# A graph layer and a mixture of experts on one core: statistics moved between folds, a table written in longer pieces, read-backs paced anew

## The chip, the cores and the metric

The kernel runs on one core of a Trainium2 chip. The metric is device time in microseconds of one execution, median of several runs. The core has five instruction streams that run beside each other and wait for one another on semaphores: TensorE (PE in the profile; PEld is its weight load), VectorE (DVE), ScalarE (ACT), GpSimd (POOL) and SyncE (SP), which here only issues DMAs. Each stream works strictly in its own order. Sixteen DMA engines move data between HBM and the on-chip memories.

## The reference, cut to what matters

```python
deg = jnp.maximum(segment_sum(ones, dst), 1.0); norm = deg ** (-0.5)
# graph layer: 6250 nodes, 106250 edges sorted by dst, 256 features
h = norm * (layernorm(x) @ W.T + b)
x = x + norm * segment_sum(h[src], dst)
# feed-forward layer: 8 experts, 256 -> 1024 -> 256, best 2 of 8 for each node
y = layernorm(x)
scores = y @ Wg.T + bg
top, idx = top_k(scores, 2);  p = softmax(top)
out = x + sum over the 2 chosen e of p_e * (relu(y @ W1[e].T + b1[e]) @ W2[e].T + b2[e])
```

The inputs are `x`, `src`, `dst` and the weights. Nothing is computed on the host; edges are only laid out as 831 chunks of 128.

## The kernel before, in words

The nodes are cut into 49 tiles of 128, tile `t` holding nodes `128 t` to `128 t + 127`, one a partition. The function `in_order` does everything; a second path, `any_order`, is taken only if a flag `g.bad` says that some assumption on the order of the edges or experts did not hold.

**First stage (lines 180 to 415), in an order written out by hand.** It makes a table `ftable` in HBM with one row of 1 KB (512 numbers in 16 bits) for each node, from which the edges are later gathered. For this it needs, of each node, mean and variance (`look(n)`, line 253: the next `n` tiles' statistics, one VectorE instruction each) and the degree. Degrees are counted on TensorE: `tally(c0, c1)` (line 268) multiplies one-hot forms of the chunks `c0` to `c1` into count tiles, one for each group of seven tiles; three such count tiles exist at a time, so a fourth waits until VectorE has copied the first away. `fold_counts(k0, k1)` (line 361) copies the counts of groups `k0` to `k1` on VectorE (`counted`) and spreads them over the partitions on TensorE (`degrees`, L296). `moments` and `columns` turn statistics and degrees into a factor and an offset for each node (VectorE, with one square root on ScalarE); `scaled(k)` applies them (ScalarE, from group 3 on partly VectorE) and rounds to 16 bits (L346, ScalarE); `rest(k)` (L349, VectorE) makes the low half of each row; `stored(k)` (L351) writes the group's 128 x 7 rows to the table with one DMA on SP, the last group with two. The tiles `tab` of three groups exist at a time.

Since TensorE and VectorE work in program order, a fold on TensorE stands behind all count matmuls of the tally written ahead of it, and whatever VectorE has next after a fold waits for it. Behind the last `rest`, VectorE makes small constants (lines 407 to 415). The memory of this stage is then reused, so the next stage's first masks wait for the last store of the table.

**Middle (lines 893 to 909).** One step `s` for each chunk of 128 edges: `gather` (L433) fetches 128 table rows with an indirect DMA on GpSimd, by the node numbers in `g.src`; VectorE makes a mask; TensorE adds the rows up (L447). Around this, at steps fixed by the tables `tasks` and `FINAL`, finished tiles are put through the linear layer, routed to two experts (`route`) and sorted into queues in HBM (`sort`, L665; `send`). The function `next_piece` puts in one piece of the feed-forward layer for each step: 56 FFN steps of 256 rows of one expert (the last five of 128). An FFN step is `up` (L780), `down` (L794) and the result `y` (L798, VectorE), written to `fyq` in HBM by SP.

**Tail (lines 910 to 996).** The same loop goes on without gathers: `read_back` (L855) fetches with an indirect DMA on GpSimd, for one tile and one of its two experts, 128 rows of results; `add_in` (L863, VectorE) adds them, 14 steps after the read or later; after some adds `store` writes four finished tiles out, from GpSimd's queue. `DONE` says how many tiles are complete after which FFN step: `(54, 46)` opens tiles up to 45 for reading once step 54 is through. A read that is opened by FFN step n waits for the writes of steps up to n alone. The table `bounds`, made from `DONE`, lets `flag` (L935) check on chip that this held for the data. `flag` counts on VectorE, sums over partitions with one matmul on TensorE (L951) 8 steps later and sets `g.bad` (L954) 4 steps after that. Tiles not opened before the last FFN step are read at the end, all reads in a row (line 990), and then added and stored one tile at a time. At last every engine loads `g.bad` and branches.

Of the kernel before, what the change touches and what calls it, by code (L numbers as in the profile page):

```python
# [10 lines left out]
I32 = mybir.dt.int32  # L11
# [4 lines left out]
OP = mybir.AluOpType  # L16
# [3 lines left out]
P = 128  # L20
N = 6250
NT = 49
# [4 lines left out]
NC = 831  # L27
# [13 lines left out]
USUAL = len(FOLLOWS) + 9  # L41
# [12 lines left out]
GROUP = 7  # L54
# [1 line left out]
SHIFT = 1.0 / 16  # L56

DONE = ((40, 31), (42, 33), (44, 34), (45, 35), (46, 37), (47, 38), (48, 39), (49, 40), (50, 42), (51, 43),
        (52, 44), (53, 45), (54, 46), (USUAL - 1, NT))
LATER = 1 << 17  # L60


# [70 lines left out]
def in_order(ctx: ExitStack, tc: tile.TileContext, g: Shared, srcT, dstT, low):  # L133
# [36 lines left out]

    most = keep.tile([P, NE], F32, name="most")
    zeros = keep.tile([P, D], F32, name="zeros")

    kept = {w: (WINDOWS[w - 1][0] % P, WINDOWS[w][0] - WINDOWS[w - 1][0]) for w in range(1, len(WINDOWS))}
    keeps = {key: keep.tile([P, 1], F32, name=f"keep{j}") for j, key in enumerate(sorted(set(kept.values())))}
# [4 lines left out]
    with (tc.manual_schedule(), tc.tile_pool(name="fdeg", bufs=2) as deg,  # L180
# [118 lines left out]
        def moments(k0, k1):  # L299

            t0, t1 = k0 * GROUP, k1 * GROUP
            n = t1 - t0
            v = deg.tile([P, 2, n], F32, name="v")
            nc.vector.tensor_scalar(v[:, 1], pds.pop(k0), 1.0, None, op0=OP.max)

            twice = deg.tile([P, n], F32, name="twice")
            nc.vector.tensor_add(twice, st[:, t0:t1, 1], st[:, t0:t1, 4])
            apart = deg.tile([P, n], F32, name="apart")
            nc.vector.tensor_sub(apart, st[:, t0:t1, 1], st[:, t0:t1, 4])
            nc.vector.scalar_tensor_tensor(apart, apart, 0.25, apart, op0=OP.mult, op1=OP.mult)  # L310
            nc.vector.tensor_add(v[:, 0], st[:, t0:t1, 2], st[:, t0:t1, 5])
            nc.vector.scalar_tensor_tensor(v[:, 0], v[:, 0], 1.0 / D, apart, op0=OP.mult, op1=OP.add)
            nc.vector.tensor_scalar(v[:, 0], v[:, 0], EPS, None, op0=OP.add)
            r = deg.tile([P, 2, n], F32, name="rs")
            nc.scalar.activation(r, v, AF.Sqrt)
            cols[k0] = twice, v, r
# [32 lines left out]
            nc.vector.tensor_sub(tab[k][:, a:b, D:2 * D], hf[k][:, a:b, :], tab[k][:, a:b, 0:D])  # L349

        def stored(k, a=0, b=GROUP):  # L351
            nc.sync.dma_start(table[(k * GROUP + a) * P:(k * GROUP + b) * P, :].rearrange("(t p) d -> p t d", p=P),
                              tab[k][:, a:b, :])


# [5 lines left out]
        def fold_counts(k0, k1):  # L361
            for k in range(k0, k1):
                counted(k)
            degrees(k0, k1)
# [3 lines left out]
        ones(256, NC)  # L368
        tally(0, 256)
        fold_counts(0, 1)  # L370
        moments(0, 1)
        look(4)
        columns(0, 1)
        scaled(0)
        tally(256, 460)
        look(10)
        fold_counts(1, 3)
        moments(1, 3)
        look(4)
        columns(1, 3)  # L380
        scaled(1)
        scaled(2)
        last_parts(0)
        tally(460, 730)
        look(10)
        fold_counts(3, 5)
        last_parts(1)
        moments(3, 5)
# [1 line left out]
        columns(3, 5)  # L390
        scaled(3)
        scaled(4)
        tally(730, NC)
        last_parts(2)
        look(7)
        fold_counts(5, 7)
        moments(5, 7)
        columns(5, 7)
# [3 lines left out]
        last_parts(4)  # L402
        last_parts(5)
        last_parts(6, ((0, 4), (4, GROUP)))


        nc.vector.tensor_scalar(g.ident, g.jp, 0.0, None, op0=OP.is_equal)
# [23 lines left out]
    def gather(c):  # L431
        rows[c] = rowpool.tile([P, 2 * D], F16, name="rows")
        nc.gpsimd.indirect_dma_start(  # L433
            out=rows[c], out_offset=None, in_=table[:, :],
            in_offset=bass.IndirectOffsetOnAxis(ap=g.src[:, c:c + 1], axis=0))

    def mask(c):
        masks[c] = work.tile([P, P], F16, name="mask", bufs=MASKS + 3)
# [454 lines left out]
    with tc.manual_schedule():  # L893
        with rowp as rowpool:
            for c in range(AHEAD):
                gather(c)
            for c in range(MASKS):
                mask(c)
            for s in range(NC):
                if s + AHEAD < NC:  # L900
                    gather(s + AHEAD)
                if s + MASKS < NC:
                    mask(s + MASKS)
                add_up(s)
                for fn, args in tasks.pop(s, []):
                    fn(*args)
                next_piece(s)
                if s % 4 == 0 and earliest.get(done + 1, NC) <= s:
                    next_piece(s)
        with tc.tile_pool(name="ftail", bufs=2) as pool:  # L910
            s = NC
            pend = []
            plan = list(DONE)
            found = list(DONE)
            got = asked = allowed = stored = 0
            latest = 0
            since = {}

            def take():
                nonlocal got, stored  # L920
                t, j, yb = pend.pop(0)[1]
                add_in(t, j, yb)
                got += 1
                if got == 2 * stored + 11:
                    store(stored, stored + 4, nc.gpsimd)
                    stored += 4

            def find():

                while found and sought > found[0][0]:  # L930
                    step, t1 = found.pop(0)
                    results(DONE[-len(found) - 2][1] if len(found) + 1 < len(DONE) else 0, t1,
                            float(P + (step + 1) * FT))

            def flag():  # L935


                late = work.tile([P, NT, 2], F32, name="late", bufs=1)
                missed = work.tile([P, 2], F32, name="missed")
                nc.vector.tensor_tensor(late, at, bounds, op=OP.is_ge)  # L940
                nc.vector.tensor_reduce(missed[:, 0:1], late, op=OP.add, axis=mybir.AxisListType.XY)
                nc.vector.tensor_reduce(missed[:, 1:2], most, op=OP.max, axis=mybir.AxisListType.X)
                nc.vector.tensor_scalar(missed[:, 1:2], missed[:, 1:2], float(SLOTS), None, op0=OP.is_gt)
                nc.vector.tensor_add(missed[:, 0:1], missed[:, 0:1], missed[:, 1:2])
                nc.vector.tensor_add(missed[:, 0:1], missed[:, 0:1], g.outside)
                ones = work.tile([P, 1], F32, name="ones")
                nc.vector.memset(ones, 1.0)
                for _ in range(8):
                    yield
                pm = psp.tile([1, 1], F32, name="pt", bufs=1)  # L950
                nc.tensor.matmul(pm, missed[:, 0:1], ones, start=True, stop=True)  # L951
                for _ in range(4):
                    yield
                nc.vector.tensor_scalar(g.bad, pm, 1.0, None, op0=OP.min)  # L954

            flagged = None
            while done < USUAL or tasks or len(plan) > 1 or asked < 2 * allowed or pend:
                for fn, args in tasks.pop(s, []):
                    fn(*args)
                if s > all_sent:  # L960
                    if chosen < min(USUAL, done + 4):
                        run(choose(chosen))
                        chosen += 1
                    elif chosen == USUAL and flagged is None:
                        flagged = True
                        in_parts(s + 1, flag)
                    if loaded2 < min(loaded1, done + 3):
                        load_second(loaded2)
                        loaded2 += 1
                    if loaded1 < min(chosen, done + (cur >= HB) + 3):  # L970
                        load_first(loaded1)
                        load_rows(loaded1)
                        loaded1 += 1
                was = done
                next_piece(s)
                if done > was:
                    since[was] = s
                find()
                if len(plan) > 1 and done > plan[0][0] and s >= since.get(plan[0][0], 0) + 4 \
                        and asked == 2 * allowed:  # L980
                    latest, allowed = plan.pop(0)
                if asked < 2 * allowed and s % (4 if s > all_sent else 2):
                    pend.append((s, read_back(pool, rowat, asked // 2, asked % 2, latest)))
                    asked += 1

                if pend and (done == USUAL or len(pend) == WAITING - 1 or s >= pend[0][0] + 14):
                    take()
                s += 1

            last = [read_back(pool, rowat, t, j) for t in range(allowed, NT) for j in range(2)]  # L990
            if stored < allowed:
                store(stored, allowed, nc.sync)
            for t, j, yb in last:
                add_in(t, j, yb)
                if j:
                    store(t, t + 1, nc.sync if t % 2 else nc.scalar)
# [495 lines left out]
```

## Time and profile before

| what | value |
|---|---|
| median of five runs (lowest, highest) | 1325.51 us (1320.11, 1327.92) |
| the profiled execution, its span | 1316.57 us, 1314.7 us |
| busy: TensorE, VectorE, GpSimd, ScalarE | 89%, 73%, 69%, 30% of the span |
| first gather, last gather | 76.6 us, 1119.6 us |
| first read-back, last read-back | 1134.99 us, 1304.48 us |
| bytes moved, mean rate | 326.02 MB, 248 GB/s |

A row of the profile's timeline gives the start and the duration in microseconds from the span's start, the engine, the line of the kernel, the operation with its output and inputs, how many instructions it merges, and in brackets how long the engine was idle before it and what ended that. A row of the windows gives, for a stretch of time, its length, the busy time of TensorE, its weight load, VectorE, ScalarE and GpSimd with the count of instructions, the granted TensorE clock, the busy share of the DMA engines and the GB/s they moved. Durations on GpSimd are rough. Names such as `rows<-ftable,src` are output and inputs.

### The profile page before, as it was taken

What the parts mean: (1) busy time and instruction counts of PE and PEld (TensorE: products, weight loads), DVE (VectorE), ACT (ScalarE), POOL (GpSimd) and SP (SyncE); (2) the same over time, 40 slices, a digit from 0 to 9 for tenths busy, and PEclk for the clock granted to TensorE, in tenths of its full rate; (3) what the DMA queues carried; (4) which work ended last, traced back from release to release, by engine and by line L of the source; (5) the groups of instructions that cost most, each with busy time, mean ns of one, the idle gap of its engine ahead of it and who ended that gap; (6) DMA issues with size and microseconds to landing.
All of it is one profiled execution on the core that took longest, in us unless ns stands there. A gap on an engine that the chain in (4) does not pass through costs nothing. (4 is left out here: it accounts for less than half of the span.)

```text
span 1314.7 us, 23752 instructions
## 1 busy us (share of the span) xinstructions
PE 1167.2 (89%) x6208; PEld 920.4 (70%) x6208; DVE 962.7 (73%) x5230; ACT 396.4 (30%) x936; POOL 900.6 (69%) x994
## 2 busy tenths in 40 slices
PE   5449886999899989999999999999999999899983
PEld 5437654767677767778777777777777777688873
DVE  7932667766878887887888887888777776875652
ACT  3712322222233232323333323333232323223221
POOL 2057777777777777777777777777777777447753
PEclk9999777999999999999999999999999999999987
DMA  9353456878788878897878787878888787689993
GB/s 321 121 158 106 121 137 206 260 244 268 242 240 275 273 234 260 258 328 253 269 249 281 240 284 225 290 233 280 274 253 289 221 289 244 222 292 399 310 351 120
DMA packets 159082, 326.02 MB, mean 248 GB/s; under 512 B 26724, under 2 KB 105528, under 8 KB 144600
## 3 DMA queue, kind: packets, MB, share of 16 engines
q1 hardware_dynamic: 111948, 196.14, 43.1%
q0 software_dynamic: 46176, 127.59, 32.9%
q8 instruction: 51, 0.84, 0.3%
q14 instruction: 95, 0.78, 0.2%
q10 hardware_dynamic: 812, 0.68, 0.2%
HBM read 268.88 MB, written 55.42 MB: 247 GB/s over the span
## 5 line engine op out<-in xcount | busy, mean ns | idle before, releaser
L433 POOL DMA_INDIRECT rows<-ftable,src x831 | 790.3, 951 | 321.8 <-issue 96.4
L780 PE MATMUL ph<-xT,w 128*128 128x256 f32 (+1 forms) x1792 | 447.1, 380 | 31.3 <-ACT xT L768 31.0
L794 PE MATMUL py<-w,hid 128*128 128x256 f32 x1712 | 431.9, 382 | 3.3 <-DVE y L798 3.3
L780 PEld LDWEIGHTS ph<-xT,w 128*128 128x128 f32 x1792 | 331.8, 195 | 104.5 <-ACT xT L768 41.0
L794 PEld LDWEIGHTS py<-w,hid 128*128 128x128 f32 x1712 | 325.6, 191 | 75.9 <-DVE y L798 3.5
L447 PE MATMUL ps<-rows,mask 128*128 128x512 f16 x831 | 320.3, 399 | 33.6 <-DMA rows<-ftable,src 29.0
L785 ACT ACTIVATE hid<-ph,w 128x256 f32<-128x256 f32 (+1 forms) x448 | 183.3, 460 | 250.3 <-PE ph L780 171.0
L440 DVE TENSOR_SCALAR mask<-col_b,rel 128x128 f16<-128x128 bf16 x831 | 207.4, 269 | 45.9 <-PE ps L447 42.3
L855 POOL DMA_INDIRECT yb<-fyq,rowat x98 | 94.8, 968 | 66.8 <-issue 26.7
L529 ACT ACTIVATE whole<-rolled 32x256 f32<-32x256 f32 (+2 forms) x156 | 64.4, 413 | 214.2 <-DVE rolled L524 213.4
L447 PEld LDWEIGHTS <-mask 128*128 128x128 f16 x831 | 87.8, 106 | 56.7 <-issue 25.6
L798 DVE TENSOR_TENSOR y<-py,w 128x256 f32<-128x256 f32 x107 | 45.3, 423 | 94.6 <-PE py L794 94.5
L521 DVE SCALAR_TENSOR_TENSOR rolled<-rolled,keep,ps 128x256 f32<-128x256 f32 x149 | 70.4, 473 | 24.3 <-PE ps L447 20.3
L863 DVE SCALAR_TENSOR_TENSOR xr<-yb,prob,xr 128x256 f32<-128x256 f32 x98 | 45.3, 482 | 49.9 <-DMA yb<-fyq,rowat 49.0
L665 PE MATMUL px<-slots,h 128*128 128x256 f32 x196 | 57.4, 418 | 17.0 <-DVE slots L644 14.6
L524 DVE TENSOR_TENSOR rolled<-ps,rolled 128x256 f32<-128x256 f32 x150 | 63.7, 424 | 5.2
L665 PEld LDWEIGHTS px<-slots,h 128*128 128x128 f32 x196 | 36.9, 201 | 36.8 <-DVE slots L644 24.5
L605 ACT ACTIVATE ex<-ex 128x1 f32<-128x1 f32 x49 | 9.9, 203 | 174.2 <-DVE ex L604 174.2
L666 ACT ACTIVATE ordered<-px 128x512 f32<-128x512 f32 x49 | 31.0, 633 | 88.0 <-issue 48.6
L552 DVE SCALAR_TENSOR_TENSOR xr<-pt,norm,xr 128x256 f32<-128x256 f32 x49 | 23.6, 482 | 42.0 <-PE pt L544 41.9
L544 PE MATMUL pt<-gw,uT 128*128 128x264 f32 x196 | 53.4, 397 | 0.0
L768 ACT ACTIVATE xT<-xs 128x512 f32<-128x512 f32 (+1 forms) x56 | 36.2, 647 | 47.2 <-DMA xs<-fhq 46.8
(183 smaller groups left out, 1133.0 us busy)
## 6 DMA issues: line engine op xcount, KB each, us to landing
w<-in_W SPq DMA_DIRECT2D x56, 1152.0 KB
w<-in_W SPq DMA_DIRECT2D x56, 1028.0 KB
fhq<-ordered SPq DMA_DIRECT2D x392, 64.0 KB
fyq<-y SPq DMA_DIRECT2D x107, 128.0 KB
rows<-ftable,src POOLq DMA_INDIRECT x831
xs<-fhq SPq DMA_DIRECT2D x51, 256.0 KB
out<-xr POOLq DMA_DIRECT2D x11, 512.0 KB
xr<-in_x SPq DMA_DIRECT2D x6, 896.0 KB
```

The costliest lines, as they stand in the source:

```text
L433: nc.gpsimd.indirect_dma_start(out=rows[c], out_offset=None, in_=table[:, :], in_offset=bass.IndirectOffsetOnAxis(ap=g.src[:, c:c + 1], ax ...
L440: nc.vector.tensor_scalar(masks[c], g.col_b[:, r:r + P], g.rel[:, c:c + 1], None, op0=OP.is_equal)
L447: nc.tensor.matmul(sums[w], masks.pop(c), rows.pop(c), start=(c == chunks[0]), stop=(c == chunks[-1]))
L521: nc.vector.scalar_tensor_tensor(new, rolled, keeps[kept[w]], ps[:, 0:D], op0=OP.mult, op1=OP.add)
L524: nc.vector.tensor_add(new, ps[:, D:2 * D], new)
L529: nc.scalar.activation(whole[t][p0:p1, :], new[p0:p1, :], AF.Copy)
L544: nc.tensor.matmul(pl, uT[:, k, :], gw[:, k, :], start=(k == 0), stop=(k == 1))
L665: nc.tensor.matmul(px[:, k, :], h2s[t][:, k * P:(k + 1) * P], slots[t], start=True, stop=True)
L780: nc.tensor.matmul(ph[:, b % 2, :n], w1[:, k * H + b * P:k * H + (b + 1) * P], f["xT"][:, k, :n], start=(k == 0), stop=(k == 1))
L785: nc.scalar.activation(f["hid"][:, b - 1 + i, :n], ph[:, i, :n], AF.Relu, bias=w1[:, 2 * H + b - 1 + i:2 * H + b + i])
L794: nc.tensor.matmul(f["py"], f["hid"][:, b, a * P:(a + 1) * P], f["w2"][:, b * D:(b + 1) * D], start=(b == 0), stop=(b == HB - 1))
L855: r = nc.gpsimd.indirect_dma_start(out=yb, out_offset=None, in_=yq[0:P + (upto + 1) * FT, :], in_offset=bass.IndirectOffsetOnAxis(ap=where ...
```

## The change

- The 49 statistics are made in other places: eight behind the first fold of counts (instead of seven ahead of the last), then 2, 6, 4, 3, 12 and 7 where there were 4, 10, 0, 4, 10 and 7.
- The second and third fold stand 20 and 30 chunks later in TensorE's order, the last tally is shorter by 30.
- The table's rows are numbered by partition first: node `128 t + p` stands in row `49 p + t`, so that one partition's seven rows of a group lie side by side. The gathers' row numbers are made from `g.src` by three VectorE instructions on 128 x 831 whole numbers, behind the last `rest`.
- While tiles are still being sorted, one read-back is issued in four steps instead of one in two.
- 47 tiles instead of 46 are opened once FFN step 54 is through.
- The flag's matmul and its last instruction stand behind the last FFN step, not in the middle of step 52.

```diff
-        (52, 44), (53, 45), (54, 46), (USUAL - 1, NT))
+        (52, 44), (53, 45), (54, 47), (USUAL - 1, NT))
...
+    rowof = keep.tile([P, NC], I32, name="rowof")
...
-            nc.sync.dma_start(table[(k * GROUP + a) * P:(k * GROUP + b) * P, :].rearrange("(t p) d -> p t d", p=P),
+            nc.sync.dma_start(table[:, :].rearrange("(p t) d -> p t d", p=P)[:, k * GROUP + a:k * GROUP + b, :],
                               tab[k][:, a:b, :])
...
         fold_counts(0, 1)
+        look(8)
         moments(0, 1)
-        look(4)
+        look(2)
         columns(0, 1)
         scaled(0)
-        tally(256, 460)
-        look(10)
+        tally(256, 480)
+        look(6)
         fold_counts(1, 3)
+        look(4)
         moments(1, 3)
-        look(4)
+        look(3)
         columns(1, 3)
         scaled(1)
         scaled(2)
         last_parts(0)
-        tally(460, 730)
-        look(10)
+        tally(480, 760)
+        look(12)
         fold_counts(3, 5)
...
-        tally(730, NC)
+        tally(760, NC)
         last_parts(2)
-        look(7)
         fold_counts(5, 7)
...
+        nc.vector.tensor_scalar(part, g.src, P - 1, None, op0=OP.bitwise_and)
+        nc.vector.tensor_scalar(part2, g.src, 7, None, op0=OP.arith_shift_right)
+        nc.vector.scalar_tensor_tensor(rowof, part, float(NT), part2, op0=OP.mult, op1=OP.add)
...
-            in_offset=bass.IndirectOffsetOnAxis(ap=g.src[:, c:c + 1], axis=0))
+            in_offset=bass.IndirectOffsetOnAxis(ap=rowof[:, c:c + 1], axis=0))
...
-                for _ in range(8):
+
+                while done < USUAL:
                     yield
                 pm = psp.tile([1, 1], F32, name="pt", bufs=1)
                 nc.tensor.matmul(pm, missed[:, 0:1], ones, start=True, stop=True)
-                for _ in range(4):
-                    yield
                 nc.vector.tensor_scalar(g.bad, pm, 1.0, None, op0=OP.min)
...
-                if asked < 2 * allowed and s % (4 if s > all_sent else 2):
+                if asked < 2 * allowed and (s % 4 if s > all_sent else s % 4 == 0):
```

## The prediction

> **What bounds the kernel now.** I read the profile's page first, then the answer on the table tile, the timeline of the first 92 us, the same stretch in 1 us windows, and the timeline of the last 200 us. The page's costliest group and the tile's answer say that GpSimd sets the length of the middle:
>
> ```profile
> L433 POOL DMA_INDIRECT rows<-ftable,src x831 | 790.3, 951 | 321.8 <-issue 96.4
> ...
> L433 POOL DMA_INDIRECT rows<-ftable,src x831: 942/946/1184, 76.6 to 1119.6; - x167
> ```
>
> 831 gathers start between 76.6 and 1119.6 us, 1.257 us apart; one is 0.946 us and the gap behind it 0.30 us (the timeline's rows), so 830 x 1.25 = 1037 of those 1043 us are plain succession. The middle can hardly shrink, but it moves as a whole with the first gather. The kernel is thus three pieces: until the first gather, 1043 us, and the tail.
>
> The first piece ends so (timeline, then windows; the last two columns of a window are the busy share of the 16 DMA engines and GB/s):
>
> ```profile
> 32.61 0.17 DVE L304 TENSOR_SCALAR v<-pd 128x14 f32<-128x14 f32 x1 [2.31 <-PE pd L296]
> ...
> 67.13 1.70 ACT L346 ACTIVATE tab<-hf 128x1792 f16<-128x1792 f32 x1 [1.48 <-DMA ftable<-tab]
> 68.86 2.09 DVE L349 TENSOR_TENSOR tab<-hf,tab 128x1024 f16<-128x1024 f32 x2 [1.02 <-ACT tab L346]
> ...
> 75.54 1.57 DVE L440 TENSOR_SCALAR mask<-col_b,rel 128x128 f16<-128x128 bf16 x9 [3.46 <-DMA ftable<-tab]
> ...
> 76.56 1.09 POOL L433 DMA_INDIRECT rows<-ftable,src  x1 [68.05 <-DVE mask L440]
> ```
> ```profile
> 67.00:68.00 1.00, 0.00 (x0) 0.00 (x0) 0.83 (x1) 0.87 (x1) 0.00 (x0) 1.00 1.03 353
> 68.00:69.00 1.00, 0.00 (x0) 0.00 (x0) 0.14 (x1) 0.82 (x1) 0.00 (x0) 1.00 1.02 328
> ...
> 74.00:75.00 1.00, 0.00 (x0) 0.00 (x0) 0.00 (x0) 0.00 (x0) 0.00 (x0) 1.00 0.94 323
> 75.00:76.00 1.00, 0.00 (x0) 0.03 (x1) 0.46 (x3) 0.00 (x0) 0.00 (x0) 1.00 0.01 2
> ```
>
> Read there: VectorE is done at 72.1 and idles 3.46 us; from 67.0 to 74.95 the DMA engines do nothing but the last 2.75 MB of the table at 346 GB/s (7.95 us). VectorE also idles 3.50 us at 22.57 and 2.31 us at 32.61 for the counts.
>
> In the tail GpSimd reads results back, each 1.25 us, and VectorE adds them in program order, so an add whose read is late holds the FFN result `y` behind it:
>
> ```profile
> 1174.53 0.81 POOL L870 DMA_DIRECT2D out<-xr  x1 [13.45 <-DVE xr L863]
> ...
> 1254.86 0.48 DVE L863 SCALAR_TENSOR_TENSOR xr<-yb,prob,xr 128x256 f32<-128x256 f32 x1 [5.43 <-DMA yb<-fyq,rowat]
> ...
> 1257.86 6.57 PE L794 MATMUL py<-w,hid 128*128 128x256 f32 x16 [3.31 <-DVE y L798]
> ...
> 1298.21 0.97 POOL L855 DMA_INDIRECT yb<-fyq,rowat  x1 [4.30 <-DMA fyq<-y]
> ...
> 1304.48 0.95 POOL L855 DMA_INDIRECT yb<-fyq,rowat  x1 [0.30 <-issue]
> ```
>
> After the last `y` has landed (1298.21) six reads follow one another, the sixth at 1304.48; its add ends at 1307.83 and the span at 1314.7.
>
> **Part 1, statistics and folds.** Same 49 statistics (0.335 us each), other places. I replay VectorE's order with the rows' durations. Eight now stand behind the first fold: 19.07 to 21.76, inside the 3.50 us idle; `v` stays at 22.57. Two instead of four before the first columns: these end 0.7 us earlier, 25.6. Six more to 27.6; the second count closes at 28.8 on TensorE, so both are folded at 29.2, and four more end at 30.6. But TensorE now runs 30 more count matmuls (0.032 us each) before it folds: `v` at 33.6, not 32.61, and VectorE idles 3.0 us there. With three instead of four statistics the columns end at 37.2 (36.5 before). Twelve instead of ten delay the fold of counts 3 and 4 to 43.5; TensorE needs that buffer for its seventh count, then has 58 instead of 28 matmuls left (2.0 us) and the fold: `v` at 46.2 (44.36). Columns end at 51.1 (49.26). Now the seven statistics that stood at 53.1 (2.38 us) are gone: counts 5 and 6 are folded at 54.97 (55.43). Net gain 0.46 us; most of the filled idle time comes back as new waits for TensorE. Bounds: 0 if a fetch gap like those at 20.09 and 26.56 (1.75 and 2.21 us, "issue") falls into the longer tally, which would make it a loss of up to 1.7; a gain of 1.5 if TensorE's 30 extra matmuls run inside such a gap.
>
> **Part 2, the table.** A partition's rows of one group are 7 KB in a piece instead of seven pieces of 1 KB, 1024 pieces instead of 6272, in eight stores on SP as before. The 1 KB stores move 346 GB/s. Nearest rows for larger pieces: 28 to 32 us, where zeros are stored in pieces of 2 KB among others, 392 to 396 GB/s; 1180 to 1200 us, weights in pieces of 8 to 9 KB, 406 GB/s, though those are loads. I take 400: 2.75 MB in 6.9 us, 1.05 us less; ends 0 (rate unchanged) and 1.3 (415). ScalarE's 1.48 us for group 3's landing shrinks by as much as that store (0.35), so the last `rest` ends near 70.0 and its store would be through by 72.1: transfer still decides. Landing 74.95 - 0.46 - 1.05 = 73.4.
> Against this speaks the Trainium skill, DMA: Bandwidth & Descriptors, "Where 436 GB/s comes from": transfers between HBM and SBUF are bound by about 358 GB/s on the HBM side. By it 1 KB pieces at 346 would be nearly at the limit and the store would gain an estimated 0.27 us. The trace disagrees: 392 to 406 GB/s in the windows named above.
>
> The three new operations (831 int32 a partition) are priced by the rows of the same shape: 0.59 (L213), 0.58 (L217), and for the two-operand one 1.02 (L211): 2.2 us, on VectorE behind the last `rest`, ahead of nine small ones of 1.2 us. 70.0 + 2.2 + 1.2 = 73.4, the moment the table lands: hidden, by the wait that was 3.46 us and is now near 0.4; uncovered it would cost up to 2.2. The gathers' own count, size and order stay, and rows are drawn at random before and after. **First gather: 1.5 us earlier (range 3 earlier to 2 later), and the middle with it.**
>
> **Part 3, pace of the read-backs.** Until the last tile is sorted one read per four steps is issued instead of one per two, six reads fewer, caught up by step 50, where before 12 slots stay empty. (i) One add (0.40) fewer stands ahead of the last `slots` on VectorE, for which TensorE waits 1.95 us at 1157.41: 0.4 gained. (ii) GpSimd, 21 reads ahead either way, is held by its first store until tile 3's add; that add now stands behind the first `y` of step 45 (1178.2 on TensorE), so the store goes at 1179.3, not 1174.53, and every later read of the same number 4.8 us later. But the `y` at 1257.39 now follows the 67th read, not the 73rd: 1240.73 + 4.4 = 1245.1 against 1249.24, 4 us earlier. TensorE's 3.31 us stall goes. (iii) Late next: reads 79 and 80 come 4.4 us later and hold step 51's `y` (1264.75) until about 1267; from there each `y` waits for reads that wait for earlier `y`. Step 52's stays at 1275, so TensorE's 3.7 us come through only in part: I put step 55's `y` (1293.73) at 1292.5, ends 1290 (TensorE alone) and 1296.
>
> **Part 4, the end.** 47 tiles instead of 46 are open before the last step: tile 46's two reads and adds go in GpSimd's free time before 1298, four reads instead of six remain: 2 x 1.26 = 2.5 us. Worked out from the reference's inputs, tile 46's last row is computed in step 53, so the flag stays 0 and the second path is not taken. The flag's matmul leaves the middle of step 52 (0.2 us of TensorE) for the end; its result is loaded by SP before the last two stores there, but is ready by 1295, and the stores wait for adds at 1297 and later: nothing.
>
> **Sum.** 1.5 + 1.2 (the last `y`) + 2.5 = 5.2 us less. The profiled execution took 1316.57 us (span 1314.7): 1311.4. Its time is 8.9 us under the median 1325.51 of five runs (1320.11 to 1327.92); on the median, 1320.3.
>
> **Rivals.**
> A, all of TensorE's time comes through: 1.5 + 3.7 + 2.5 = 7.7, 1317.8. For it: at full pace step 55 would end at 1290. Against: reads 43 and 44 hold the `y` of steps 54 and 55.
> B, the front gains nothing because the stores stay at 346 GB/s: the 1.05 us are lost, the 2.2 us of address arithmetic stay covered, and 0.5 or nothing is left there and 2.5 at the end, 1322.5 to 1323. For it: 1 KB reads of the input come at 321 GB/s, near the stores, so the size of a piece may not be what limits. Against: the 2 KB rows. The rule of the Trainium skill named above, that the HBM side binds, would lead here. A fetch gap in the longer tally does the same to the sum, up to 1325.
> C, slower: the loop `y`, write, read, add, `y` two steps on. From step 51 to 53 it took 1264.75 to 1284.30, 19.5 us, against 14.3 us for two steps of TensorE; only the next turn (9.4) caught up. If step 51's `y` comes at 1267 and the second turn takes 19.5 as well, step 55's comes at 1306: 12.3 late, less 2.5 and 1.5, 8 slower, 1333.8. It decides once a turn exceeds 17.
>
> **Chances.** Likeliest 0.50, A 0.20, B 0.16, C 0.14. About 0.5% (6.6 us) is what a measurement of this kernel can tell from no change; the runs of one kernel themselves spread over 7.8 us. Half of A and a third of the likeliest, moved by that spread, fall below 1318.9, with the wider ends of parts 1 and 2: faster 0.31. C and a little of B: slower 0.16. The rest, 0.53, within. The likeliest alone spans 1315 to 1326; the range takes in A's lower end with the spread (1312) and stops short of most of C (1330).
>
> **What would show it.** Last landing of the table near 73.4, 1 us windows there near 400 GB/s; first gather near 75.1; `v` of the second fold later (33.6), of the last earlier; no TensorE stall for `y` near 1255; GpSimd's first store near 1179; four reads behind the last write. Wrong it would be by stores still at 346 GB/s, by a VectorE wait no longer for the table but for itself ahead of the masks, or by `y` of steps 53 to 55 later than before.

## The result, and the profile after

The changed kernel takes 1313.30 us (median of 49 runs, 1307.21 to 1330.10) against 1320.13 us (median of 91 runs of the kernel before, 1310.52 to 1334.42): 0.9957 of the time, 95% interval 0.9945 to 0.9969, so some 5.7 us or 0.43% faster. The forecast was 5.2 us less. That the sum fits says little, as will be seen: the terms behind it do not all hold.

The profiled execution of the changed kernel took 1317.82 us (span 1316.0), which is 4.5 us above its median; that of the kernel before took 1316.57 us, 3.6 us under its own. Set beside each other, the two profiles would show a loss. They are therefore compared by stretches, and each stretch against the profiles of the experiments too.

The costliest group of the page and the answer on the table's tile give, as before, the length of the middle:

```profile
L440 POOL DMA_INDIRECT rows<-ftable,rowof x831 | 789.6, 950 | 319.9 <-issue 96.6
...
L440 POOL DMA_INDIRECT rows<-ftable,rowof x831: 942/946/1188, 75.5 to 1117.0; - x167
```

The gathers start 1.1 us earlier (75.5, not 76.6) and are as long as they were. What leads there, in the timeline, and the 1 us windows of the same stretch (last two columns: busy share of the DMA engines, GB/s):

```profile
33.55 0.17 DVE L305 TENSOR_SCALAR v<-pd 128x14 f32<-128x14 f32 x1 [3.30 <-PE pd L297]
...
46.03 0.17 DVE L305 TENSOR_SCALAR v<-pd 128x14 f32<-128x14 f32 x1 [0.33 <-PE pd L297]
...
56.75 1.70 ACT L347 ACTIVATE tab<-hf 128x1792 f16<-128x1792 f32 x1
...
58.35 0.21 ACT L316 ACTIVATE rs<-v 128x28 f32<-128x28 f32 x1
58.59 0.33 DVE L324 RECIPROCAL rt<-rs 128x28 f32<-128x28 f32 x1 [1.25 <-ACT rs L316]
...
66.93 1.70 ACT L347 ACTIVATE tab<-hf 128x1792 f16<-128x1792 f32 x1 [0.92 <-DMA ftable<-tab]
...
74.46 1.57 DVE L447 TENSOR_SCALAR mask<-col_b,rel 128x128 f16<-128x128 bf16 x9 [0.51 <-DMA ftable<-tab]
75.48 1.10 POOL L440 DMA_INDIRECT rows<-ftable,rowof  x1 [66.98 <-DVE mask L447]
```
```profile
68.00:69.00 1.00, 0.00 (x0) 0.00 (x0) 0.54 (x2) 0.63 (x1) 0.00 (x0) 1.00 1.03 409
69.00:70.00 1.00, 0.00 (x0) 0.00 (x0) 1.00 (x2) 0.00 (x0) 0.00 (x0) 1.00 1.00 416
...
73.00:74.00 1.00, 0.00 (x0) 0.00 (x0) 0.89 (x8) 0.00 (x0) 0.00 (x0) 1.00 0.84 332
74.00:75.00 1.00, 0.00 (x0) 0.10 (x1) 0.54 (x4) 0.00 (x0) 0.00 (x0) 1.00 0.00 0
```

The same 16 DMA engines are as busy as before (shares near 1.0), but move 387 to 418 GB/s in the full windows. The table has landed at about 73.85, by the share of 0.84 in the window that starts at 73. VectorE's wait for it is 0.51 us instead of 3.46. New is the 1.25 us wait at 58.59: ScalarE's root (0.21 us) stands behind the rounding of group 4, which ScalarE began at 56.75.

The tail, from the timeline:

```profile
1182.38 0.81 POOL L877 DMA_DIRECT2D out<-xr  x1 [16.68 <-DVE xr L870]
...
1271.81 0.93 DVE L870 SCALAR_TENSOR_TENSOR xr<-yb,prob,xr 128x256 f32<-128x256 f32 x2 [3.94 <-DMA yb<-fyq,rowat]
1272.66 0.42 DVE L805 TENSOR_TENSOR y<-py,w 128x256 f32<-128x256 f32 x1
...
1273.13 3.72 PE L801 MATMUL py<-w,hid 128*128 128x256 f32 x16 [1.34 <-DVE y L805]
...
1286.94 3.98 PE L787 MATMUL ph<-xT,w 128*128 128x128 f32 x32 [2.42 <-ACT xT L775]
...
1295.08 0.94 POOL L862 DMA_INDIRECT yb<-fyq,rowat  x1 [1.82 <-DMA fyq<-y]
...
1301.26 0.97 POOL L862 DMA_INDIRECT yb<-fyq,rowat  x1 [0.30 <-DVE xr L870]
...
1305.04 0.95 POOL L862 DMA_INDIRECT yb<-fyq,rowat  x1 [0.30 <-POOLq L1456]
```

The stall of TensorE near 1255 is gone, but step 51's `y`, predicted near 1267, starts at 1272.66, behind two adds that waited 3.94 us for their reads, and TensorE now waits there (1.34) and at 1286.94 (2.42). Four reads remain at the end, as said; but the first of them follows an idle time of only 0.30 us, the plain succession of GpSimd. It starts 5.6 us after the last `y` (1295.68) because GpSimd is still busy with earlier reads and a store, and not because it waits for that `y` to land, as the first of the six did before (4.30 us at 1298.21). These earlier reads, of tiles 45 and 46, are no backlog: GpSimd waited 1.82 us at 1295.08 for the results of step 54 that open them, and the last `y` came 0.6 us after that.

### The profile page after: what moved, and what is told of

It reads as the page before. It is cut to its first block, busy times and chain, and to the rows that moved or that the text cites. A ratio compares the mean times of both kernels' runs of the same rounds, so it can differ in the third digit from the quotient of the medians.

```text
span 1316.0 us, 23755 instructions
## 1 busy us (share of the span) xinstructions
PE 1170.7 (89%) x6208; PEld 921.4 (70%) x6208; DVE 966.8 (73%) x5233; ACT 396.4 (30%) x936; POOL 900.1 (68%) x994
## 5 line engine op out<-in xcount | busy, mean ns | idle before, releaser
L440 POOL DMA_INDIRECT rows<-ftable,rowof x831 | 789.6, 950 | 319.9 <-issue 96.6
L787 PE MATMUL ph<-xT,w 128*128 128x256 f32 (+1 forms) x1792 | 451.7, 383 | 32.2 <-ACT xT L775 32.0
L801 PEld LDWEIGHTS py<-w,hid 128*128 128x128 f32 x1712 | 323.2, 190 | 73.4 <-DVE y L805 2.0
```

The source lines that it names most:

```text
L440: nc.gpsimd.indirect_dma_start(out=rows[c], out_offset=None, in_=table[:, :], in_offset=bass.IndirectOffsetOnAxis(ap=rowof[:, c:c + 1], ax ...
L787: nc.tensor.matmul(ph[:, b % 2, :n], w1[:, k * H + b * P:k * H + (b + 1) * P], f["xT"][:, k, :n], start=(k == 0), stop=(k == 1))
L801: nc.tensor.matmul(f["py"], f["hid"][:, b, a * P:(a + 1) * P], f["w2"][:, b * D:(b + 1) * D], start=(b == 0), stop=(b == HB - 1))
```

## The experiments

All ratios are to the kernel before, run side by side on the same chip; differences between two kernels run side by side are of their means, with a 95% interval from the scatter of their runs. The stretches of the profiles on chips of like speed, in us (the last five `y` are those of steps 51 to 55, and two `y` belong to each step ahead of these):

| kernel | first gather | to second `y` of step 48 | to `y` of 51 | to `y` of 55 | to end of span |
|---|---|---|---|---|---|
| before | 76.56 | 1149.2 | 39.0 | 29.0 | 21.0 |
| changed | 75.48 | 1151.7 | 45.4 | 23.0 | 20.3 |
| after_2 (changed, again) | 75.77 | 1148.0 | 47.2 | 22.2 | 20.0 |
| u_table | 76.93 | 1144.2 | 47.0 | 23.3 | 20.0 |
| u_stats | 75.42 | 1147.2 | 47.4 | 24.1 | 20.6 |
| u_done | 75.78 | 1148.7 | 47.6 | 22.9 | 20.1 |
| e_early2 | 70.38 | 1149.3 | 46.9 | 22.6 | 20.0 |
| u_pace (old pace) | 75.76 | 1148.2 | 41.0 | 25.1 | 18.5 |
| pace_2 (old pace, again) | 75.49 | 1146.8 | 40.3 | 25.7 | 18.7 |
| e_both (old pace) | 70.35 | 1146.6 | 38.3 | 26.3 | 19.1 |

The third column scatters by 7 us between kernels that do nearly the same there. TensorE's granted clock differs from execution to execution (0.87 in the profile before and 0.85 in the one after from 100 to 300 us, 0.93 and 0.95 from 1110 to 1180), which may be the reason. The timed runs point the same way: over those of the changed kernel (0.951 to 0.966) a mean granted clock lower by 0.001 goes with about 1.0 us more, and the two profiled executions had 0.962 (before) and 0.957 (changed). That the clock causes the scatter is not shown. Where the first stage is the same, the first gather itself varies by 0.3 us (75.48 to 75.78, and from 75.21 to 75.75 on the slower chip further down). The columns behind the third repeat within 1 to 3 us and show two clear families among the changed kernels, the new pace and the old.

**Each part undone by itself.** First the layout of the table (rows of a tile together, pieces of 1 KB, node numbers used as they are, and the three instructions for the places left out):

```diff
-  table[:, :].rearrange("(p t) d -> p t d", p=P)[:, k * GROUP + a:k * GROUP + b, :]
+  table[(k * GROUP + a) * P:(k * GROUP + b) * P, :].rearrange("(t p) d -> p t d", p=P)
...
-  ap=rowof[:, c:c + 1]
+  ap=g.src[:, c:c + 1]
```

> The changed kernel with the table's rows laid as before (1 KB pieces, gathers by g.src, none of the three new VectorE operations). Theory: the longer pieces are worth the whole gain of the first piece, so the last 2.75 MB go at 346 GB/s again instead of about 400, land near 75.2 instead of 73.8, and the first gather starts at 76.6 to 76.8 (75.48 in the changed kernel, 76.56 before). Time 1.1 us above the changed kernel, ratio to the kernel before about 0.9965. Rival (the table is worth nothing, VectorE sets the end of this piece): first gather within 0.3 of 75.5, ratio 0.9957.

Measured: 1313.09 us, 0.9972 (0.9948 to 0.9997). In its timeline the wait for the table is back to what it was before the change, and the first gather is 1.45 us later than in the changed kernel:

```profile
75.91 1.57 DVE L442 TENSOR_SCALAR mask<-col_b,rel 128x128 f16<-128x128 bf16 x9 [3.46 <-DMA ftable<-tab]
```

So the longer pieces are worth 1.45 us at the first gather, ScalarE's shorter wait included (0.92 us, against 1.47 here).

Then the statistics and folds, put back as in the kernel before:

```diff
-        look(8)
         moments(0, 1)
-        look(2)
+        look(4)
...
-        tally(256, 480)
-        look(6)
+        tally(256, 460)
+        look(10)
         fold_counts(1, 3)
-        look(4)
         moments(1, 3)
-        look(3)
+        look(4)
...
-        tally(480, 760)
-        look(12)
+        tally(460, 730)
+        look(10)
...
-        tally(760, NC)
+        tally(730, NC)
         last_parts(2)
+        look(7)
```

> The changed kernel with statistics and folds in the old places, the rest new. Theory: part 1 gives nothing or a little loss, because the time it fills comes back as waits for TensorE and, in the changed kernel's trace, as 1.25 us for ScalarE's square root, which stands behind group 4's rounding: first gather at 75.2 to 75.6 (75.48 with part 1), ratio the changed kernel's 0.9957 within 0.0015. Rival (my recorded 0.46 us): first gather at 75.9 or later.

Measured: 1310.02 us, 0.9941 (0.9917 to 0.9966). The first gather starts at 75.42, against 75.48 with the new places: they gain nothing. Its reciprocal waits 0.29 us for the root, where the changed kernel's waits 1.25:

```profile
58.51 0.33 DVE L324 RECIPROCAL rt<-rs 128x28 f32<-128x28 f32 x1 [0.29 <-ACT rs L316]
...
75.42 1.09 POOL L439 DMA_INDIRECT rows<-ftable,rowof  x1 [66.96 <-DVE mask L446]
```

Against the kernel before, which has the same places and the short pieces, this is 1.14 us earlier: a second reading of what the longer pieces are worth.

The pace of the reads:

```diff
-  if asked < 2 * allowed and (s % 4 if s > all_sent else s % 4 == 0):
+  if asked < 2 * allowed and s % (4 if s > all_sent else 2):
```

> The changed kernel with one read-back in two steps while tiles are still sorted, as before. Theory: TensorE's stall for y near step 51 (3.31 us before, 0 in the changed kernel) comes back with 2.5 to 4 us, and the last y comes 1 to 2 us later after the first read: ratio 0.9965 to 0.9975. Rival (the pace is worth nothing because the chain of y, write, read and add decides): stall back but the last y at the same distance, ratio 0.9957.

Measured: 1309.28 us, 0.9927 (0.9897 to 0.9957): not over the changed kernel but under it. My expectation missed. TensorE's stall for step 50 is back, and it is the only one; the row of the waits of TensorE from 1230 us to the end is one line:

```profile
PE py L801 <- DVE y L805: 3.0, 1, 3.0
```

The number of tiles opened before the last step:

```diff
-  (52, 44), (53, 45), (54, 47), (USUAL - 1, NT))
+  (52, 44), (53, 45), (54, 46), (USUAL - 1, NT))
```

> The changed kernel with 46 instead of 47 tiles open before the last step. Theory: six reads instead of four behind the landing of the last y, 2.5 us later at the end: from the last y's addition to the span's end 21.0 us as before (1293.73 to 1314.7) against 20.3 in the changed kernel's profiled execution, where GpSimd was still busy when it landed, so 0.7 to 2.5 us, ratio 0.9962 to 0.9976. Rival (all of the tail's gain is here): ratio 0.998 or more.

Measured: 1313.24 us, 0.9973 (0.9942 to 1.0005). Six reads are left after the last `y`, and still the stretch from there to the end is 20.1 us, as with four (20.0 to 20.6). At the new pace, then, the two reads fewer are worth nothing. The first of the six starts 3.37 us after the last `y` (1294.92), and GpSimd was free for only 0.41 us ahead of it, where the kernel before had waited 4.30 us:

```profile
1298.29 0.97 POOL L862 DMA_INDIRECT yb<-fyq,rowat  x1 [0.41 <-issue]
```

**The old pace once more, beside the changed kernel on one chip,** and with both an earlier fold. The expectations call the second `y` of step 48 "step 46's"; the figures are right, the name is wrong.

> The changed kernel once more, beside the three others on one chip. Expected ratio to the kernel before 0.9957 (its 49 runs gave 0.9945 to 0.9969), first gather at 75.5 us, VectorE's columns of groups 5 and 6 waiting over 1 us for ScalarE's square root, and in the tail waits of TensorE for y of 1 us and more somewhere among steps 51 to 55.

Measured: 1312.98 us, 0.9969 (0.9944 to 0.9993); first gather 75.77, reciprocal's wait 1.25 us, TensorE waiting 2.06 us for step 51's `y`.

> The changed kernel with the old pace of the tail's reads (every step but each second one, instead of each fourth one, until the last send). Theory 'the new pace costs': about 0.3% under the changed kernel on the same chip (0.992 to 0.994 of the kernel before), one wait of TensorE of about 3 us for step 51's y and none after it, step 55's y not later than in the changed kernel. Rival 'the pace is worth nothing either way and the earlier figure was scatter': within 0.1% of the changed kernel. The recorded working (the new pace gains 1.2 us): 0.1% over it.

Measured: 1309.98 us, 0.9938 (0.9917 to 0.9959); 4.0 us (1.3 to 6.8) under after_2 on the same chip. The earlier figure was no scatter: the new pace costs some 4 us. Where, the table shows: step 51's `y` comes 38 to 41 us after the second `y` of step 48 with the old pace and 45 to 48 with the new one; 2 to 3 us of that are won back by step 55 (25 to 26 us from step 51, against 22 to 24), and the end is 1.5 us longer. By the first `y` of step 50 GpSimd has begun 78 reads with the old pace and 71 to 73 with the new one; 5 to 7 reads at 1.25 us make 6 to 9 us, the size of the delay. The timeline of pace_2 shows GpSimd caught up and waiting for results at 1258.71, and `y` of step 51 behind an add that also waits for its read (2.67 us), but 8 us earlier than in after_2:

```profile
1258.71 0.97 POOL L862 DMA_INDIRECT yb<-fyq,rowat  x1 [2.03 <-DMA fyq<-y]
...
1262.23 0.48 DVE L870 SCALAR_TENSOR_TENSOR xr<-yb,prob,xr 128x256 f32<-128x256 f32 x1 [2.67 <-DMA yb<-fyq,rowat]
1262.63 0.42 DVE L805 TENSOR_TENSOR y<-py,w 128x256 f32<-128x256 f32 x1
```

In the changed kernel GpSimd's reads follow one another at 0.30 us from 1235 to 1272, broken only by its stores; the first that waits longer for a result is at 1276.56.

Folding earlier. Tallies end where group 2 and group 4 are complete, the looks are divided again, and group 4 is scaled and rounded behind the root:

```diff
-        tally(256, 480)
+        tally(256, 364)
         look(6)
         fold_counts(1, 3)
-        look(4)
+        look(2)
...
-        tally(480, 760)
-        look(12)
+        tally(364, 603)
+        look(14)
...
-        scaled(4)
-        tally(760, NC)
+        tally(603, NC)
         last_parts(2)
         fold_counts(5, 7)
         moments(5, 7)
+        scaled(4)
```

> The changed kernel, but counts folded earlier than in either kernel: the tallies end at chunks 364 and 603 instead of 480 and 760, looks divided again (6, 2, 3, 14, 7), and group 4 scaled and rounded on ScalarE after the square root of groups 5 and 6 instead of ahead of it. Theory: VectorE's order is what sets the table, and its own waits (3.30 us for the second fold, 1.25 us for the square root) are what can be had: v of the second fold near 29.5 instead of 33.55, wait of the reciprocal under 0.4, first gather near 71.5 (70.5 to 73) instead of 75.5, and the ratio 0.3% under the changed kernel's, 0.992 to 0.994. Rival 'the rows of the table come from ScalarE and the queue in any case, or TensorE has no chunk tallied in time': first gather 74.5 or later, ratio that of the changed kernel.

Measured: 1307.80 us, 0.9917 (0.9886 to 0.9948); 6.1 us (3.1 to 9.2) under after_2. In its timeline neither the second fold nor the root is waited for any more, and the masks no longer wait for the table but only for VectorE:

```profile
29.59 0.17 DVE L305 TENSOR_SCALAR v<-pd 128x14 f32<-128x14 f32 x1
...
53.53 0.32 DVE L324 RECIPROCAL rt<-rs 128x28 f32<-128x28 f32 x1
...
69.38 1.56 DVE L447 TENSOR_SCALAR mask<-col_b,rel 128x128 f16<-128x128 bf16 x9
...
70.38 1.11 POOL L440 DMA_INDIRECT rows<-ftable,rowof  x1 [61.87 <-DVE mask L447]
```

The first gather is 5.1 us earlier than in the changed kernel, a little better than the range given. By the last gather only 1.4 to 1.7 us of that are left in the profiled execution (1115.57 against 1116.98 and 1117.25): the gathers themselves took 792.5 us in all against 789.6 in after_2, while their waits behind the first gather are nearly the same (253.6 and 252.9 us). The second `y` of step 48 comes 4.1 us earlier than in after_2 (1219.64, 1223.77), and the span ends 4.1 us earlier. The gain in the timed runs is 3 us at least.

> The early folds of the run before together with the old pace of the reads; all else as in the changed kernel (table layout, four last reads, flag). If both theories hold, the two gains add, since one lies ahead of the first gather and the other behind the last: 0.6% under the changed kernel, ratio 0.989 to 0.991. If the pace is worth nothing, 0.992 to 0.994. If what the front gains is lost again before the last send, no lower than the old pace alone.

Measured: 1302.59 us median, 0.9901 (0.9865 to 0.9938): the fastest of all, faster than both kernels; 9.3 us (5.3 to 13.2) under the changed kernel on the same chip, 5.2 (1.6 to 8.9) under pace_2. That is near the sum of the two gains, 4.0 and 6.1, one in front of the first gather and one behind the last. Against e_early2 alone it is 3.1 us (-0.7 to 6.9, six runs of each), which these runs do not tell from nothing.

**Four more, on another chip,** on which everything takes a fifth longer (the kernel before 1584.61 us, median of 23; more on that at the end). The first 76 us are as long there as elsewhere; the rest is read from ratios to the kernel before on that chip and by comparing these four with each other.

Later adds at the new pace:

```diff
-  if pend and (done == USUAL or len(pend) == WAITING - 1 or s >= pend[0][0] + 14):
+  if pend and (done == USUAL or len(pend) == WAITING - 1 or s >= pend[0][0] + 20):
```

> The changed kernel with the new pace of the reads, but each read is added in at the earliest 20 steps after it is asked for instead of 14. In the seven profiled executions with the new pace step 51's y comes 45 to 47 us after step 46's (38 to 41 with the old pace), behind two adds on VectorE that wait 2 to 4 us for their reads. Theory 'the reads put off until after the last send keep GpSimd busy without a pause, and VectorE, in its order, waits for them ahead of y': with the adds later, y of step 51 comes 41 us or less after step 46's, TensorE's wait of 1.3 to 2.3 us for it is gone, and the last y comes 66 to 67 us after step 46's instead of 69 to 71; the stretch from the last y to the end stays at 20 us, since GpSimd has the same reads to make. Ratio 0.993 to 0.995. Rival 'y is late because its weights or its input are late': step 51's y 45 us or more after step 46's all the same.

Measured: 1568.18 us, 0.9908 (0.9879 to 0.9937), and 7.2 us (3.1 to 11.2) under the next kernel, which keeps the 14 steps and has the flag's product at its old place. The size is larger than expected, but not at the place that was named (the expectation speaks of seven profiles with the new pace; the table has six): on this chip step 51's `y` came 45.8 us after the second `y` of step 48, where the three others, which keep 14 steps, have 41.4 to 42.2. It was that earlier `y` that came sooner (145.3 us after the last gather, 152.8 to 161.4 in the others). From the second `y` of step 48 to the end it took 93.4 us, the three others 88.2 to 88.9. That adds placed later help is measured; that they help at step 51 is not: in this one profile they did not, and the three others show no such delay there on this chip.

The flag's product put back to its old place:

```diff
-                while done < USUAL:
+                for _ in range(8):
                     yield
                 pm = psp.tile([1, 1], F32, name="pt", bufs=1)
                 nc.tensor.matmul(pm, missed[:, 0:1], ones, start=True, stop=True)
+                for _ in range(4):
+                    yield
```

> The changed kernel with the flag's product at its old place, 8 and 4 steps on, among the last steps. The recorded working gives the move nothing: within 0.2% of the changed kernel (0.995 to 0.998 of the kernel before), stretch from step 46's y to the last one 68.5 to 71.5 us as in the changed kernel. Rival 'the flag's product stood in TensorE's way': 1 us more or above.

Measured: 1574.83 us, 0.9953 (0.9925 to 0.9982), within the interval of the changed kernel. From the second `y` of step 48 to the last one it took 71.1 us, against 70.0 and 70.1 in the next two kernels, which keep the new place; that is inside the scatter of this stretch. The move is worth nothing that can be measured.

One instruction moved, with `rounded(k)` the last two lines of `scaled(k)`, which leaves them out for group 4:

```diff
         moments(5, 7)
+        rounded(4)
         columns(5, 7)
```

> The changed kernel, with one instruction moved: ScalarE rounds group 4 after the square root of groups 5 and 6 instead of ahead of it. If the 1.25 us at which VectorE's reciprocal stands is that rounding (1.70 us on ScalarE in front of the root), the wait falls to 0.4 or less, columns of groups 5 and 6 end at 59.4 as the prediction had it instead of 60.25, and the first gather starts at 74.6 instead of 75.5. If the rounding is only put off and comes back at the last pieces, the wait falls and the first gather stays at 75.3 or later.

Measured in its timeline:

```profile
57.12 0.23 ACT L316 ACTIVATE rs<-v 128x28 f32<-128x28 f32 x1 [0.66 <-DVE v L314]
57.25 1.68 ACT L351 ACTIVATE tab<-hf 128x1792 f16<-128x1792 f32 x1
57.38 0.33 DVE L324 RECIPROCAL rt<-rs 128x28 f32<-128x28 f32 x1 [0.29 <-ACT rs L316]
...
74.25 1.10 POOL L445 DMA_INDIRECT rows<-ftable,rowof  x1 [65.78 <-DVE mask L452]
```

The root is now ahead of the rounding, the wait is 0.29 instead of 1.25 us, and the first gather starts at 74.25, where x_take20, with the same fold times (`v` at 56.01 and 56.02) and the old order, has 75.21: 0.96 us, all that the wait shrank by. (One timed run; its total of 1574.76 says nothing at this size.)

The three instructions for the rows' places (lines 409 to 411) done three times over:

```diff
         nc.vector.scalar_tensor_tensor(rowof, part, float(NT), part2, op0=OP.mult, op1=OP.add)
+        nc.vector.tensor_scalar(part, g.src, P - 1, None, op0=OP.bitwise_and)
...
+        nc.vector.scalar_tensor_tensor(rowof, part, float(NT), part2, op0=OP.mult, op1=OP.add)
```

> The changed kernel with the three instructions that work out the rows' places made three times over (4.4 us more of VectorE, same values). In the changed kernel they end 0.5 us before the table has landed. If that is their cover and nothing else hides them, the first gather starts 3.8 to 3.9 us later, at 79.3, and the time rises by up to 0.3%. If VectorE has other slack there, the first gather stays at 75.5.

Measured: first gather at 77.86, 2.65 us later than x_take20's 75.21, for 4.36 us more work (one timed run, 1568.84 us). The direction is that of the theory, the cover is wider: not 0.5 but 1.7 us. The order on VectorE is not the same as in the changed kernel: the first mask stands ahead of four of the small constants, and the gather starts 0.42 us after it instead of 1.02:

```profile
77.36 0.16 DVE L424 TENSOR_SCALAR head<-col_f 128x8 f32<-128x8 f32 x1
77.44 0.25 DVE L453 TENSOR_SCALAR mask<-col_b,rel 128x128 f16<-128x128 bf16 x1
77.60 0.16 DVE L425 COPY filled<-head 128x8 f32<-128x8 f32 x1
```

## Why the prediction was right or wrong

**Part 1 (0.46 us gained): wrong.** The times of the replay hold to 0.2 us as far as 56.3: `v` of the second fold 33.55 for 33.6, of the third 46.03 for 46.2, counts 5 and 6 folded at 54.83 for 54.97. The step that failed is what comes next: the columns were to end near 59.4, reckoned from VectorE alone, and end at 60.25. The columns of groups 3 and 4 came 1.7 us later than before, as reckoned, and `scaled(4)` on ScalarE with them, so that the rounding of group 4 now stood in front of the root. A 0.46 us gain on one engine met a second engine's order. u_stats shows the part worth nothing, x_sqrt shows the place of this one instruction worth 0.96 us.

**Part 2 (1.05 us by the rate, 400 GB/s): right.** 387 to 418 GB/s in the full windows, and 1.45 us at the first gather with the new places of the statistics (u_table against the changed kernel), 1.14 with the old ones (u_stats against the kernel before); the two differ by about as much as the first gather varies, and the end given was 1.3. ScalarE's wait for a free tile shrank by 0.56 us (1.48 before, 0.92 now), not by the 0.35 reckoned. That the rows' places are covered holds too. With part 1 worth nothing the landing is at 73.85 instead of 73.4, and the first gather at 75.48 instead of 75.1. The rule of the Trainium skill that stood against this part (DMA: Bandwidth & Descriptors, "Where 436 GB/s comes from", about 358 GB/s) is not borne out by these windows: they are stores from on-chip memory to HBM, at 409 and 416 GB/s. Rival B falls with them.

**Part 3 (0.4 + 1.2 us): wrong in sign.** Step (i), 0.4 us, cannot be seen: TensorE's wait was 1.95 us before, and is 1.2 to 2.0 with the new pace and 2.3 and 1.4 with the old one (u_pace, pace_2). Step (ii) came about: GpSimd's first store goes at 1177.4 to 1182.4 with the new pace, at 1171.1 and 1173.0 with the old one (4 to 9 us later on the same chip, where 4.8 was reckoned), and the stall near 1255 is gone. Step (iii) failed by its size: reads 79 and on were to hold step 51's `y` until 1267, 2.3 us later; in the profiles with the new pace it came 6 us and more later, measured from step 48. The reckoning moved each read by the 4.8 us of the store that held them, and then let GpSimd catch up; but its reads stand shoulder to shoulder at 1.25 us until 1272, so six reads put off come back as some 6 times 1.25 us where an add stands in front of a `y`. That the pace costs this is shown, twice, by putting the old one back; that it comes about in just this way is read from the rows, and the one kernel that moved the adds (x_take20) did not confirm it. Rival C's loop is not what happened: from 1230 us to step 51's `y` no read waits more than the usual 0.30 us for a write, from step 51 to 53 it took 12.8 us, under the 17 at which the rival was to decide, and from 51 to 55 the changed kernel needed 23.0 us against 29.0 before. From the second `y` of step 48 to the end it needs 88.7 and 89.4 us, the kernel before 89.0, and the change with the old pace 84.6 and 84.7.

**Part 4 (2.5 us): right with the old pace, nothing with the new one.** From the last `y` to the end it takes 21.0 us with six reads and the old pace (before), 18.5, 18.7 and 19.1 with four (u_pace, pace_2, e_both): 1.9 to 2.5. No kernel with the old pace has six reads and the rest of the change, so this rests on the one profile of the kernel before. With the new pace it takes 20.1 with six (u_done) and 20.0 to 20.6 with four. The term was worked out as if GpSimd had 4.30 us free ahead of the last landing. With the new pace it had 0.41 (u_done), mainly because the last `y` follows step 54's, which opens the reads of tiles 45 and 46, after 3.7 to 4.3 us, where it was 6.3 before and 4.9 with the old pace. The two parts were summed as if they were independent.

**The sum.** 5.2 us were forecast and 5.7 measured, but of this the profiles show 0.8 to 1.1 us at the first gather (75.48 and 75.77, against 76.56) and about nothing in the tail. The other 4 to 5 us are not found. That the sum comes out is luck: part 1 gave nothing, parts 3 and 4 together about nothing instead of 3.7 us, because the pace costs some 4, and the gain that makes up for them has no known place. On the chip of after_2 the change was worth 4.1 us (0.9969). One profile of the kernel before stands against these, from an execution 3.6 us faster than its median, and the stretch from the first gather to step 48 scatters by 7 us; a gain of some us in the middle, or an unusually short tail in that one profile, would not be seen. Of the parts undone one by one none gives the missing us back: without the table layout, the new `DONE` or the flag's place the kernel is at 0.9972, 0.9973 and 0.9953, all with the changed kernel's 0.9957 in their intervals. Adding single parts to the kernel before would have told more and was not tried.

## What to carry to other kernels

When an order written out by hand is moved on one engine, replay the neighbour's queue as well: here a root of 0.21 us behind a rounding of 1.70 us ate the gain, and moving one instruction gave 0.96 us. Work that is put off on an engine which later runs without a pause can come back at its full length where something waits for it in order, as the rows here suggest, so a stall removed is only a gain if that engine has idle time between the two places. And two savings at the same queue are not to be added up: the reads saved at the end were worth 2.5 us or nothing, by whether that queue had idle time to take them ahead of the last landing.

## What the runs showed of the hardware

Stores of the table in pieces of 7 KB ran at 387 to 418 GB/s against 323 to 353 with pieces of 1 KB, with the DMA engines equally busy by their records (shares of 0.94 to 1.04); I had taken 400 from rows of other transfers.

One chip of those used ran every kernel a fifth slower: the kernel before 1573.28 to 1599.56 us in 23 runs, with a mean granted clock of TensorE of 0.90 to 0.92 where the others show 0.94 to 0.97. The first 76 us are the same there (first gather at 75.21 in x_take20 and 75.75 in u_flag, at 75.42 to 75.78 elsewhere). The gathers' group among the groups by line, first of u_flag on that chip, then of the changed kernel on another (count, busy us, mean ns, idle before and what ended it):

```profile
L440 POOL DMA_INDIRECT rows<-ftable,rowof x831 | 791.1, 952 | 525.8 <-issue 176.6 <-PE ps L454 175.8 <-DVE mask L447 67.2
```
```profile
L440 POOL DMA_INDIRECT rows<-ftable,rowof x831 | 789.6, 950 | 319.9 <-issue 96.6 <-DVE mask L447 67.0 <-PE ps L454 62.1
```

A gather takes as long (952 and 950 ns); it is the idle time in front that is 526 us instead of 320, partly behind TensorE's sums, partly with no cause that the profile names. What slows that chip was not looked into. The ratio of u_flag there, 0.9953, is near the changed kernel's 0.9957 elsewhere.
